# Output turned by VectorE in 32 by 32 blocks instead of by TensorE, with a reordered start and a last sum in halves

## The chip, the cores and the metric

The kernel runs on one core of one Trainium2 chip. The metric is the device time of one execution in microseconds (us), the median of several runs. Three runs of the kernel before took 2236.97, 2237.91 and 2240.64 us; the median is 2237.91 us. In the profiles PE is TensorE's matrix multiply, PEld its weight load, DVE is VectorE, ACT is ScalarE, POOL is GpSimd and SP is SyncE, whose queue here carries most of the transfers.

## The reference, cut to what matters

The input `x` has 32 batches of 512 nodes with 256 features, `adj` has a 512 by 512 mask of zeros and ones for each batch. All is float32.

```
h = relu(layernorm(x))                        # per node, over 256 features
# branch 1: convolution along the nodes
c = relu(bn1(conv1(h)))                       # 1 tap, 256 -> 256
x_conv = relu(bn2(conv2(c)) + h)              # 17 taps, 256 -> 256
# branch 2: messages over a graph
s = h @ w_se.T + b_se                         # 3 numbers per node
A = exp(-|s_n - s_m|^2) * adj
x_nmp = A @ relu(h @ w_msg.T + b_msg)
# gates
x_in = concat(x_conv, x_nmp)                  # 512 features
gi, gh = x_in @ w_ih.T + b_ih,  h @ w_hh.T + b_hh    # three parts each: r, z, n
r = sigmoid(gi_r + gh_r);  z = sigmoid(gi_z + gh_z)
n = tanh(gi_n + r * gh_n)
out = x + (1 - z) * n + z * h
```

## The kernel before, in words

**Layout.** Nearly everything is held turned: features on the 128 partitions (so two halves, d or o = 0 and 1), the 512 nodes along the free axis. The input arrives with nodes on partitions; after the layer norm `norm_t` turns it by TensorE (`turn`, a multiplication with an identity matrix) into `hT`, which is also stored to `HD` in DRAM and fetched again when other stages need it (`hTg` for the graph, `hTb` for the gates, `hT` for a later first convolution).

**Stages per batch.** `norm`: VectorE's statistics, `rsqrt` with a power on GpSimd, `shift` on VectorE, then ScalarE scales the input in place. `norm_t`, then `conv1` into the array `h1`. `convolution`: the 17 taps for a group of 4 batches, as 25 products with transformed weights; the weights are made once, in the first group, from `conv2_w` by `weights_first` on VectorE and ScalarE, and stored to `WD`; later groups fetch them. Operands come from `operand_some` on VectorE. `graph`: `messages`, `kernel_exp`, `masked` (which turns the mask: by TensorE for the first 8 batches; for the others the mask is loaded in 32 by 32 blocks, already moved to their places, and VectorE transposes each block), `gather`. `gates`: four accumulations in PSUM for each half o (`ps_r`, `ps_h`, `ps_z`, `ps_n`), and at the end the mixing of `n`, `z` and `hT` (`mix`, `mix_next`, `mix_last`), which leaves the batch's result, features on partitions, in `o_sb`.

**The output.** `finish` (line 764) takes two of the four blocks of 128 nodes at a time: four `turn`s into one PSUM bank bring nodes back to the partitions, VectorE adds the residual `x` that `load_res` (line 774) has fetched, and SP stores 256 KB in runs of 1 KB. That is 8 turns, 2 additions, 2 stores and 2 residual loads for a batch.

**What sets the order.** The schedule is written out by the program itself. Each stage is a generator in `streams`; a planner keeps a clock `now` of TensorE's planned time and estimates of when VectorE and ScalarE get free (`dve.free`, `act.free`), and always continues the stream that lies furthest back by its own clock. `fill` puts VectorE's background work between (norms, operands, weights, sums), and `LATER` holds small steps with due times. Each engine then runs its instructions in exactly the order in which they were issued, and so does SP's queue with its transfers: an instruction that waits holds up everything behind it on that engine. Before the planner starts, some things are issued outright: the input of batch 0, small vectors, weights, then `bn_affine` twice (scales of the batch norms), then `load(0)`, `load(1)` and so on, which put the norms of the first four batches into `NORMS`, then the convolution weights and the first masks. Weight preparation may begin when the planned clock passes `prepare_at`, 16 there.

Of the kernel before, what the change touches and what calls it, by code (L numbers as in the profile page):

```python
# [8 lines left out]
F32 = mybir.dt.float32  # L9
# [4 lines left out]
P = 128  # L14
# [30 lines left out]
def kernel(  # L45
# [49 lines left out]

    now = 10.0
    LAG = 0.6

    def elements(t):
# [22 lines left out]
    def matmul(ps, lhsT, rhs, **more):  # L124
        nonlocal now
        now += max(0.22, elements(ps) / 600.0)
        nc.tensor.matmul(ps, lhsT, rhs, **more)  # L127

    def turn(ps, a):
        nonlocal now  # L130
        now += 0.11
        nc.tensor.transpose(ps, a, ident)  # L132
# [5 lines left out]
    def bank():  # L138
        return gps.tile([P, N], F32, name="ps_g")
# [4 lines left out]
    def later(t, f):  # L144
        LATER.append((t, f))
        LATER.sort(key=lambda e: e[0])

    def settle():
        while LATER:
            LATER.pop(0)[1]()  # L150


    XS, HT, HB, HR, HG, XN, XR = {}, {}, {}, {}, {}, {}, {}
    NORMS, NORM_AT = {}, {}
    HD = {b: dram.tile([P, ND, N], F32, name=f"hd{b}") for b in range(B)}
    ND_ = {(b, d): dram.tile([P, N], F32, name=f"nd{b}_{d}") for b in range(B) for d in range(ND)}
    begun = 0

    def fetch(b, xs=None):
        XS[b] = front.tile([P, NT, D], F32, name="x_sb", bufs=2) if xs is None else xs  # L160
        nc.sync.dma_start(XS[b], x[b].rearrange("(c p) d -> p c d", p=P))

    def load(b, xs=None):
        if b not in XS:
            fetch(b, xs)
        NORMS[b] = norm(b)
        NORM_AT[b] = now + 7.0 if b >= G else 0.0

    def load_row(b):
        HR[b] = front.tile([P, ND, N], F32, name="hT", bufs=2)  # L170
# [16 lines left out]
            nc.sync.dma_start(XN[b, d], ND_[b, d])  # L187

    fetch(0)
    vec = const.tile([P, _NCOL], F32)  # L190
    nc.sync.dma_start(vec, vecs)
    w1 = const.tile([P, ND, D], F32)
# [7 lines left out]


    wmsg = const.tile([P, ND, D + 3], F32)
    nc.sync.dma_start(wmsg[:, :, :D], w_msg)
    nc.sync.dma_start(wmsg[:, :, D:], w_se)
    bmsg = const.tile([P, D + 3], F32)
    nc.sync.dma_start(bmsg[:, :D], b_msg.to_broadcast([P, D]))
    nc.sync.dma_start(bmsg[:, D:], b_se.rearrange("k o -> o k").to_broadcast([P, 3]))
    ident = const.tile([P, P], F32)
    make_identity(nc, ident)
    mhalf = const.tile([P, 4], F32)  # L210
# [394 lines left out]
                freed = len(X2) // 25  # L605
        return True

    prepare, prepare_at = weights_first(), 16.0

    def prepare_some():  # L610
        nonlocal prepare_at
# [149 lines left out]
        act.activation(sums, ps, AF.Copy)  # L761
        nc.scalar.dma_start(ND_[b, d], sums)

    def finish(b, o_sb, c):
        ps = bank()
        for j in range(2):
            for d in range(ND):
                at = (j * ND + d) * P
                turn(ps[:, at : at + P], o_sb[:, d, (c + j) * P : (c + j + 1) * P])
        y = XR.pop((b, c))  # L770
        dve.tensor_tensor(y, ps.rearrange("p (j d) -> p j d", j=2), y, op=ALU.add)
        nc.sync.dma_start(out[b].rearrange("(c p) d -> p c d", p=P)[:, c : c + 2, :], y)

    def load_res(b):
        for c in range(0, NT if b < B else 0, 2):
            XR[b, c] = late.tile([P, 2, D], F32, name="res", bufs=2)
            nc.sync.dma_start(XR[b, c], x[b].rearrange("(c p) d -> p c d", p=P)[:, c : c + 2, :])

# [54 lines left out]
    def gates(b):  # L835

        load_gates(b)
        load_sums(b, 0)
        load_sums(b, 1)
        hT = HB[b]  # L840
        o_sb = late.tile([P, ND, N], F32, name="o_sb")
        x_in = []

        def cols(o, g):
            return slice(g * D + o * P, g * D + (o + 1) * P)

        def products(ps, o, g, first, last, of, then=None):


            sources = ((whh, 0), (wih, 0), (wih, ND))  # L850
            for k in range(first, last):
                w, at = sources[k]
                for i in range(ND):
                    matmul(
                        ps, w[:, at + i, cols(o, g)], hT[:, i, :] if k == 0 else x_in[2 * k - 2 + i],
                        start=(k == of[0] and i == 0), stop=(k == of[1] and i == ND - 1),
                    )
                if k == last - 1 and then is not None:
                    then()
                yield now  # L860

        def residual():
            xconv = XC.pop(b)[:, :, :N]
            dve.tensor_tensor(xconv, xconv, hT, op=ALU.add)
            yield dve.free + 0.3
            act.activation(xconv, xconv, AF.Relu)
            x_in.extend([xconv[:, i, :] for i in range(ND)] + [XN[b, d] for d in range(ND)])

        def mix_next(r, z, o):
            act.activation(  # L870
                r, r, AF.Tanh,
                bias=vec[:, _COL["b_ih"] + 2 * ND + o : _COL["b_ih"] + 2 * ND + o + 1],
            )
            later(act.free + 0.3, lambda: mix_last(r, z, o))

        def mix_last(r, z, o):
            t = o_sb[:, o, :]
            dve.tensor_tensor(t, hT[:, o, :], r, op=ALU.subtract)
            dve.tensor_tensor(t, z, t, op=ALU.mult)
            dve.tensor_tensor(t, r, t, op=ALU.add)  # L880
            if o == ND - 1:
                unfinished[b] = o_sb

        for o in range(ND):
            r = z = None

            def reset():
                nonlocal r
                settle()
                r = late.tile([P, N], F32, name="r")  # L890
                act.activation(r, ps_r, AF.Sigmoid, bias=brz[:, o : o + 1])

            def reset_hidden():
                dve.scalar_tensor_tensor(
                    r, ps_h, vec[:, _COL["b_hh"] + 2 * ND + o : _COL["b_hh"] + 2 * ND + o + 1], r,
                    op0=ALU.add, op1=ALU.mult,
                )

            def update():
                nonlocal z  # L900
                z = late.tile([P, N], F32, name="z")
                act.activation(z, ps_z, AF.Sigmoid, bias=brz[:, ND + o : ND + o + 1])

            def mix():
                dve.tensor_tensor(r, ps_n, r, op=ALU.add)
                later(dve.free + 0.3, lambda r=r, z=z, o=o: mix_next(r, z, o))
                if o == ND - 1:
                    load_sums(b + 1, 0)
                    load_sums(b + 1, 1)

            ps_r = acc.tile([P, N], F32, name="ps_acc")
            if o == 0:
                yield lambda: b in evacuated
                yield evacuated[b]
                yield from residual()
                yield from products(ps_r, o, 0, 0, 1, (0, 2))
                yield act.free + LAG
            else:
                yield from products(ps_r, o, 0, 0, 1, (0, 2))
            yield from products(ps_r, o, 0, 1, 3, (0, 2), reset)  # L920
            ps_h = acc.tile([P, N], F32, name="ps_acc")
            yield from products(ps_h, o, 2, 0, 1, (0, 0), reset_hidden)
            ps_z = acc.tile([P, N], F32, name="ps_acc")
            yield from products(ps_z, o, 1, 0, 3, (0, 2), update)
            if o == 0:
                load_gates(b + 1)
            ps_n = acc.tile([P, N], F32, name="ps_acc")
            yield from products(ps_n, o, 2, 1, 3, (1, 2), mix)
        gated.add(b)

    unfinished = {}

    def all_finishes():
        for b in range(B):
            yield lambda: b in unfinished
            yield dve.free + LAG
            for c in range(0, NT, 2):
                finish(b, unfinished[b], c)
                yield now
            load_res(b + 1)  # L940


    bn1_sc, bn1_sh = bn_affine("bn1")
    bn2_sc, bn2_sh = bn_affine("bn2")
    brz = const.tile([P, 2 * ND], F32)
    dve.tensor_tensor(
        brz, vec[:, _COL["b_ih"] : _COL["b_ih"] + 2 * ND], vec[:, _COL["b_hh"] : _COL["b_hh"] + 2 * ND],
        op=ALU.add,
    )

    turn_of = 0

# [58 lines left out]

    def all_gates():
        yield lambda: late is not None
        load_res(0)
        for b in range(B):
            yield from gates(b)

# [1 line left out]


    streams = {
        "finish": (all_finishes(), 1e9, -2.0),
        "rows": (all_rows(), 1e9, -2.0),
        "begins": (all_begins(), 4.2, -0.15),
        "graphs": (all_graphs(), 49.0, 0.0),
# [5 lines left out]
    hold = {name: None for name in streams}  # L1031

    load(0)
    load(1)
    spare = front.tile([P, NT, N], F32, name="at", bufs=1).rearrange("p c (k d) -> p (c k) d", d=D)
    for b in (2, 3):
        load(b, spare[:, (b - 2) * NT : (b - 1) * NT, :])
    for k0, k1 in ((0, 9), (9, TAPS)):
        for c in range(ND):
            nc.sync.dma_start(wflat[:, c, k0 + 1 : k1 + 1, :], conv2_w[:, c, k0:k1, :])  # L1040
    gr.ask(3)

# [72 lines left out]
```

## Time and profile before

| what | before |
|---|---|
| median of three runs | 2237.91 us |
| the profiled execution, whole | 2241.54 us |
| its span, first to last instruction | 2239.7 us |
| TensorE busy | 2154.9 us (96%) |
| VectorE busy | 1450.3 us (65%) |
| ScalarE busy | 787.7 us (35%) |
| mean granted TensorE clock | 0.989 |
| DMA: packets, of them under 512 bytes | 328,270, 214,160 |
| first matrix work on TensorE | at 15.1 us |
| first product of the convolution | at 69.2 us |

Busy time is the time in which an engine executes something; where TensorE's work is queued densely, its records overlap. A row of a group gives line, engine, operation, output and inputs, shapes and count, then busy time and mean, then the idle time of that engine just before and who ended it. Since nearly all instructions are issued through helpers, one line (L118) stands for all of VectorE and ScalarE, L127 for all matmuls and L132 for all turns; the names of the tiles tell them apart.

### The profile page before, as it was taken

The numbers are of one execution on the slowest core, as the hardware profiler recorded it, in microseconds if no ns is written. First come the engines' busy times: TensorE is split into PE (matmuls) and PEld (weight loads), VectorE is DVE, ScalarE is ACT, GpSimd is POOL, SyncE is SP. The second block draws the span as 40 slices with busy tenths as digits, with TensorE's granted clock in tenths as the row PEclk, the third lists the DMA queues.
The fourth block names the chain that finished last, engine by engine and source line by source line (L and its number), as shares of the span: only waits on it lengthen the run. The fifth ranks groups of instructions, "written<-read, shape, count | busy, mean of one in ns | idle before, by whom it ended". The sixth has DMA issues, their size and how long they took to land. (4 is left out here: it accounts for less than half of the span.)

```text
span 2239.7 us, 26162 instructions
## 1 busy us (share of the span) xinstructions
PE 2154.9 (96%) x9640; PEld 1346.7 (60%) x9640; DVE 1450.3 (65%) x2700; ACT 787.7 (35%) x1322; POOL 56.7 (3%) x73
## 2 busy tenths in 40 slices
PE   4899899999999999999999999999999999999998
PEld 2777766566655666566665655656666566665443
DVE  4687876666657667568764667747767467676222
ACT  4545532424333342234432343332432324222311
POOL 1000000000000000000000000000000000000000
PEclk9999999999999999999999999999999999999999
DMA  6344645445555455444555445545544544453121
GB/s 237 132 143 178 248 172 190 137 151 157 165 165 160 138 171 178 149 140 151 185 161 182 127 142 161 176 166 174 156 150 151 150 151 145 147 169 85 61 75 37
DMA packets 328270, 342.40 MB, mean 153 GB/s; under 512 B 214160, under 2 KB 263696, under 8 KB 327504
## 3 DMA queue, kind: packets, MB, share of 16 engines
q1 hardware_dynamic: 308720, 287.52, 41.7%
q10 hardware_dynamic: 17424, 46.67, 5.4%
q0 software_dynamic: 2000, 6.56, 0.8%
q8 instruction: 76, 1.25, 0.2%
q14 instruction: 50, 0.41, 0.1%
HBM read 270.68 MB, written 69.99 MB: 152 GB/s over the span
## 5 line engine op out<-in xcount | busy, mean ns | idle before, releaser
L127 PE MATMUL ps_acc<-xconv,wih 128*128 128x512 f32 x768 | 362.4, 594 | 5.2 <-ACT xconv L118 5.2
L127 PE MATMUL ps_acc<-xnb,wih 128*128 128x512 f32 x768 | 363.9, 596 | 0.0
L127 PE MATMUL ps_acc<-hTb,whh 128*128 128x512 f32 x768 | 357.7, 594 | 2.8 <-ACT r L118 2.7
L127 PE MATMUL ps_c<-xd,w 128*128 128x116 f32 x2800 | 342.1, 275 | 0.0
L127 PEld LDWEIGHTS ps_c<-xd,w 128*128 128x128 f32 x2800 | 328.4, 192 | 5.1 <-issue 4.8
L118 DVE TENSOR_TENSOR r<-ps_acc,r 128x512 f32<-128x512 f32 x64 | 44.2, 691 | 392.6 <-PE ps_acc L127 392.6
L127 PEld LDWEIGHTS ps_acc<-xconv,wih 128*128 128x128 f32 x768 | 140.8, 190 | 160.3 <-issue 150.0
L127 PEld LDWEIGHTS ps_acc<-xnb,wih 128*128 128x128 f32 x768 | 140.4, 190 | 156.4 <-issue 155.6
L127 PE MATMUL ps_g<-at,msg 128*128 128x512 f32 x512 | 229.2, 596 | 3.7 <-DVE at L118 3.7
L127 PEld LDWEIGHTS ps_acc<-hTb,whh 128*128 128x128 f32 x768 | 140.3, 190 | 150.2 <-issue 139.0
L127 PEld LDWEIGHTS ps_b<-x,w 128*128 128x128 f32 x1400 | 182.9, 193 | 72.2 <-issue 57.2
L127 PE MATMUL ps_b<-x,w 128*128 128x116 f32 x1400 | 184.9, 275 | 9.4 <-DVE w L118 5.1
L118 ACT ACTIVATE mid<-ps_b 128x232 f32<-128x232 f32 x175 | 63.6, 364 | 318.8 <-PE ps_b L127 301.4
L127 PEld LDWEIGHTS ps_g<-at,msg 128*128 128x128 f32 x512 | 95.7, 191 | 114.7 <-issue 107.4
L118 DVE SCALAR_TENSOR_TENSOR x<-x,x 128x480 f32<-128x480 f32 (+1 forms) x184 | 143.9, 782 | 3.0
L127 PE MATMUL ps_g<-hT,w 128*128 128x512 f32 x256 | 122.5, 622 | 22.1 <-ACT hT L118 11.4
L127 PE MATMUL ps_g<-wmsg,hTg 128*128 128x259 f32 x512 | 131.8, 389 | 4.8 <-ACT h L118 4.5
L118 DVE TENSOR_TENSOR x<-x 128x240 f32<-128x240 f32 (+1 forms) x320 | 134.3, 461 | 0.4
L118 DVE SCALAR_TENSOR_TENSOR r<-ps_acc,vec,r 128x512 f32<-128x512 f32 x64 | 48.0, 750 | 123.3 <-PE ps_acc L127 108.2
L127 PEld LDWEIGHTS ps_g<-wmsg,hTg 128*128 128x128 f32 x512 | 96.5, 194 | 47.2 <-issue 29.7
L118 ACT ACTIVATE h<-ps_g,bn_shift,bn_scale 128x252 f32<-128x252 f32 (+1 forms) x192 | 81.0, 495 | 119.2 <-PE ps_g L127 118.0
L118 DVE TENSOR_TENSOR msg<-ps_g,bmsg 128x256 f32<-128x256 f32 x128 | 53.5, 419 | 103.6 <-PE ps_g L127 103.2
(101 smaller groups left out, 2437.3 us busy)
## 6 DMA issues: line engine op xcount, KB each, us to landing
w<-wd SPq DMA_DIRECT2D x150, 768.0 KB, 5.2
m_sb<-in_adj_dram SPq DMA_DIRECT2D x384, 64.0 KB, 2.5
hd<-hT ACTq DMA_DIRECT2D x32, 512.0 KB, 4.9
hTg<-hd SPq DMA_DIRECT2D x32, 512.0 KB, 4.5
res<-in_x_dram SPq DMA_DIRECT2D x64, 256.0 KB, 3.2
hTb<-hd SPq DMA_DIRECT2D x32, 512.0 KB, 5.9
xnb<-nd SPq DMA_DIRECT2D x64, 256.0 KB, 2.8
out_dram<-res SPq DMA_DIRECT2D x64, 256.0 KB, 2.3
```

Source lines behind the costliest of these rows:

```text
L118: getattr(self.engine, name)(*tiles, **more)
L127: nc.tensor.matmul(ps, lhsT, rhs, **more)
```

## The change

The output is no longer turned by TensorE. `leave` replaces `finish`: for each half o, VectorE transposes the 128 by 512 result within blocks of 32 by 32, adds the residual, and four transfers store it, each moving 32 partitions with runs of 128 bytes (32 features of one node). The residual is loaded in the same arrangement, four transfers for each half, into a ring of three buffers. The blocks' order along the rows is set by the DRAM side of these transfers. `r` has two buffers now, `o_sb` holds one half instead of two.

At the start, the input of batch 1 is asked for right behind that of batch 0; the whole norm of batch 0 is issued before the `bn_affine` scales; message weights are asked for after the inputs of the first four batches; the two parts of the convolution weights come in another order; the planner's clock begins at 5 and weight preparation may begin at 26 instead of 16.

At the end, the last accumulation of the last batch (`ps_n`, o = 1) is done in two halves of 256 columns, and mixing, transposing and storing are done for each half.

```diff
-    now = 10.0
+    now = 5.0
...
+    ARRIVES = (0.0, 7.0, 11.0, 13.0)
...
-        NORM_AT[b] = now + 7.0 if b >= G else 0.0
+        NORM_AT[b] = now + 7.0 if b >= G else ARRIVES[b]
...
     fetch(0)
+    fetch(1)
...
-    prepare, prepare_at = weights_first(), 16.0
+    prepare, prepare_at = weights_first(), 26.0
...
-    def finish(b, o_sb, c):
-        ps = bank()
-        for j in range(2):
-            for d in range(ND):
-                at = (j * ND + d) * P
-                turn(ps[:, at : at + P], o_sb[:, d, (c + j) * P : (c + j + 1) * P])
-        y = XR.pop((b, c))
-        dve.tensor_tensor(y, ps.rearrange("p (j d) -> p j d", j=2), y, op=ALU.add)
-        nc.sync.dma_start(out[b].rearrange("(c p) d -> p c d", p=P)[:, c : c + 2, :], y)
...
+    XB = x.rearrange("b (k i) d -> b i k d", i=32)
+    OB = out.rearrange("b (k i) d -> b i k d", i=32)
+
+    def blocks(t, dram_b, o, store):
+        for g in range(P // 32):
+            at = o * P + 32 * g
+            a = t[32 * g : 32 * g + 32, :].rearrange("i (k j) -> i k j", j=32)
+            d = dram_b[:, :, at : at + 32]
+            nc.sync.dma_start(*((d, a) if store else (a, d)))
+
+    def load_res(b, o):
+        if b < B and (b, o) not in XR:
+            XR[b, o] = late.tile([P, N], F32, name="res", bufs=3)
+            blocks(XR[b, o], XB[b], o, False)
...
+        def mix_last(r, z, o, s):
+            if s.start == 0:
+                parts.append(late.tile([P, N], F32, name="o_sb"))
+            t = parts[-1]
+            dve.tensor_tensor(t[:, s], hT[:, o, s], r[:, s], op=ALU.subtract)
+            dve.tensor_tensor(t[:, s], z[:, s], t[:, s], op=ALU.mult)
+            dve.tensor_tensor(r[:, s], r[:, s], t[:, s], op=ALU.add)
+            later(dve.free, lambda: leave(r, t, o, s))
+
+        def leave(r, t, o, s):
+            dve.transpose(t[:, s], r[:, s])
+            y = XR[b, o]
+            dve.tensor_tensor(y[:, s], t[:, s], y[:, s], op=ALU.add)
+            for g in range(P // 32):
+                at = slice(32 * g, 32 * g + 32)
+                nc.sync.dma_start(
+                    OB[b][:, s.start // 32 : s.stop // 32, o * P + 32 * g : o * P + 32 * g + 32],
+                    y[at, s].rearrange("i (k j) -> i k j", j=32),
+                )
+            if s.stop == N:
+                del XR[b, o]
+                load_res(b + 1, o)
...
-                r = late.tile([P, N], F32, name="r")
+                r = late.tile([P, N], F32, name="r", bufs=2)
...
-            yield from products(ps_n, o, 2, 1, 3, (1, 2), mix)
+            if b < B - 1 or o < ND - 1:
+                yield from products(ps_n, o, 2, 1, 3, (1, 2), mix)
+                continue
+
+            for h in range(2):
+                s = slice(h * N // 2, (h + 1) * N // 2)
+                for j in range(2 * ND):
+                    matmul(
+                        ps_n[:, s], wih[:, j, cols(o, 2)], x_in[j][:, s],
+                        start=(j == 0), stop=(j == 2 * ND - 1),
+                    )
+                mix(s)
+                yield now
+            settle()
...
     load(0)
+    while 0 in NORMS:
+        NORM_AT[0] = next(NORMS[0], -1.0)
+        if NORM_AT[0] < 0.0:
+            del NORMS[0]
+    bn1_sc, bn1_sh = bn_affine("bn1")
+    bn2_sc, bn2_sh = bn_affine("bn2")
...
+    NORM_AT[0] = act.free + LAG
     load(1)
...
+    nc.sync.dma_start(wmsg[:, :, :D], w_msg)
...
-    for k0, k1 in ((0, 9), (9, TAPS)):
-        for c in range(ND):
+    for c in range(ND):
+        for k0, k1 in ((0, 9), (9, TAPS)):
             nc.sync.dma_start(wflat[:, c, k0 + 1 : k1 + 1, :], conv2_w[:, c, k0:k1, :])
```

More of the change, by code (lines that the diff above doesn't have):

```diff
@@ L202 @@
     wmsg = const.tile([P, ND, D + 3], F32)
-    nc.sync.dma_start(wmsg[:, :, :D], w_msg)
-    nc.sync.dma_start(wmsg[:, :, D:], w_se)
     bmsg = const.tile([P, D + 3], F32)
-    nc.sync.dma_start(bmsg[:, :D], b_msg.to_broadcast([P, D]))
-    nc.sync.dma_start(bmsg[:, D:], b_se.rearrange("k o -> o k").to_broadcast([P, 3]))
     ident = const.tile([P, P], F32)
@@ L762, in gather @@
         nc.scalar.dma_start(ND_[b, d], sums)
-    def finish(b, o_sb, c):
-        ps = bank()
-        for j in range(2):
-            for d in range(ND):
-                at = (j * ND + d) * P
-                turn(ps[:, at : at + P], o_sb[:, d, (c + j) * P : (c + j + 1) * P])
-        y = XR.pop((b, c))
-        dve.tensor_tensor(y, ps.rearrange("p (j d) -> p j d", j=2), y, op=ALU.add)
[L772 to L777, printed above, removed]
+    XB = x.rearrange("b (k i) d -> b i k d", i=32)
[10 more added lines that the diff above has]
+            blocks(XR[b, o], XB[b], o, False)
     def begin(b):
@@ L840, in gates @@
         hT = HB[b]
-        o_sb = late.tile([P, ND, N], F32, name="o_sb")
+        parts = []
         x_in = []
@@ L867, in residual, with mix_next @@
             x_in.extend([xconv[:, i, :] for i in range(ND)] + [XN[b, d] for d in range(ND)])
-        def mix_next(r, z, o):
+        def mix_next(r, z, o, s):
             act.activation(
-                r, r, AF.Tanh,
+                r[:, s], r[:, s], AF.Tanh,
                 bias=vec[:, _COL["b_ih"] + 2 * ND + o : _COL["b_ih"] + 2 * ND + o + 1],
             )
[L874 to L882, printed above, removed]
+            later(act.free + 0.3, lambda: mix_last(r, z, o, s))
+        def mix_last(r, z, o, s):
[19 more added lines that the diff above has]
+                load_res(b + 1, o)
         for o in range(ND):
@@ L902, in update, with mix @@
                 act.activation(z, ps_z, AF.Sigmoid, bias=brz[:, ND + o : ND + o + 1])
-            def mix():
-                dve.tensor_tensor(r, ps_n, r, op=ALU.add)
-                later(dve.free + 0.3, lambda r=r, z=z, o=o: mix_next(r, z, o))
+            def mix(s=slice(0, N)):
+                dve.tensor_tensor(r[:, s], ps_n[:, s], r[:, s], op=ALU.add)
+                later(dve.free + 0.3, lambda r=r, z=z, o=o: mix_next(r, z, o, s))
                 if o == ND - 1:
@@ L927, in gates @@
             ps_n = acc.tile([P, N], F32, name="ps_acc")
-            yield from products(ps_n, o, 2, 1, 3, (1, 2), mix)
-        gated.add(b)
[L931 to L949, printed above, removed]
+            if b < B - 1 or o < ND - 1:
[11 more added lines that the diff above has]
+            settle()
+        gated.add(b)
     turn_of = 0
@@ L1013, in all_gates @@
         yield lambda: late is not None
-        load_res(0)
+        for o in range(ND):
+            load_res(0, o)
         for b in range(B):
@@ L1021 @@
     streams = {
-        "finish": (all_finishes(), 1e9, -2.0),
         "rows": (all_rows(), 1e9, -2.0),
@@ L1033 @@
     load(0)
+    while 0 in NORMS:
[4 more added lines that the diff above has]
+    bn2_sc, bn2_sh = bn_affine("bn2")
+    brz = const.tile([P, 2 * ND], F32)
+    dve.tensor_tensor(
+        brz, vec[:, _COL["b_ih"] : _COL["b_ih"] + 2 * ND], vec[:, _COL["b_hh"] : _COL["b_hh"] + 2 * ND],
+        op=ALU.add,
+    )
+    NORM_AT[0] = act.free + LAG
     load(1)
@@ L1037 @@
         load(b, spare[:, (b - 2) * NT : (b - 1) * NT, :])
-    for k0, k1 in ((0, 9), (9, TAPS)):
-        for c in range(ND):
+    nc.sync.dma_start(wmsg[:, :, :D], w_msg)
+    nc.sync.dma_start(wmsg[:, :, D:], w_se)
+    nc.sync.dma_start(bmsg[:, :D], b_msg.to_broadcast([P, D]))
+    nc.sync.dma_start(bmsg[:, D:], b_se.rearrange("k o -> o k").to_broadcast([P, 3]))
+    for c in range(ND):
+        for k0, k1 in ((0, 9), (9, TAPS)):
             nc.sync.dma_start(wflat[:, c, k0 + 1 : k1 + 1, :], conv2_w[:, c, k0:k1, :])
```

## The prediction

> **What bounds the kernel now.** First the page: span and busy shares; then the table of stages, the groups with shapes kept apart, the chain that ended last, and the timeline of the start.
>
> ```profile
> span 2239.7 us, 26162 instructions
> PE 2154.9 (96%) x9640; PEld 1346.7 (60%) x9640; DVE 1450.3 (65%) x2700; ACT 787.7 (35%) x1322; POOL 56.7 (3%) x73
> 0.00:69.20 69.20, 34.74 (x109) 19.41 (x110) 31.86 (x100) 36.22 (x74) 10.27 (x22) 0.92 0.57 215
> 69.20:130.00 60.80, 55.26 (x402) 49.60 (x401) 46.67 (x99) 25.26 (x43) 2.31 (x2) 0.95 0.35 126
> 130.00:280.00 150.00, 138.87 (x891) 111.61 (x891) 125.33 (x228) 75.03 (x139) 7.36 (x10) 0.97 0.56 200
> 700.00:2097.00 1397.00, 1379.22 (x6066) 849.28 (x6065) 930.48 (x1697) 483.54 (x790) 17.30 (x14) 1.00 0.50 153
> ```
>
> The stage rows give the stretch, its length, then busy PE, weight load, VectorE, ScalarE, GpSimd, clock, DMA share, GB/s. From 700 to 2097 us TensorE lacks 18 of 1397 us: work taken off TensorE there is time saved. In the first 69.2 us it lacks 34.5, and no other engine is full: that stage is waits.
>
> Groups by shape (busy, mean ns | idle before), then two pieces of the chain:
>
> ```profile
> L132 PE MATMUL ps_g<-ident,o_sb 128*128 128x128 f32 x256 | 33.3, 272 | 3.6 <-DVE o_sb L118 3.6
> L118 DVE STREAM_TRANSPOSE right<-m_sb 128x512 f32<-128x512 f32 x96 | 67.6, 704 | 27.8 <-PE ps_g L734 22.3 <-DMA hTb<-hd 3.5 <-issue 1.8
> 2169.14 0.87 PE ps_g L132 x8
> 2202.47 0.87 PE ps_g L132 x8
> ```
>
> The timeline of the start (start, length, [idle before]), then a row of the DMA issues (KB each, us to land) and one of SP's waits:
>
> ```profile
> 14.44 2.07 ACT L118 ACTIVATE x_sb<-x_sb,shift,rstd 128x256 f32<-128x256 f32 x4 [8.60 <-DVE shift L118]
> 23.02 1.76 DVE L118 SCALAR_TENSOR_TENSOR g<-wraw 128x1536 f32<-128x1536 f32 x1 [8.61 <-DMA wraw<-in_conv_w_dram]
> 26.49 0.15 DVE L118 SCALAR_TENSOR_TENSOR shift<-mv,rstd 128x4 f32<-128x4 f32 x1
> 28.30 5.08 PE L127 MATMUL ps_g<-hT,w 128*128 128x512 f32 x8 [10.40 <-ACT hT L118]
> 69.23 12.24 PE L127 MATMUL ps_c<-x,w 128*128 128x116 f32 x96
> m_sb<-in_adj_dram SPq DMA_DIRECT2D x384, 64.0 KB, 2.5
> SPq L772 <- DVE res L118: 263.6, 39, 28.8
> ```
>
> To see: the 256 output turns; eight of them take 0.87 us of the chain; the same 32-block transpose already runs on VectorE for masks (704 ns); VectorE's queue stood behind a convolution weight not yet landed (23.02) while batch 1's `shift` waited behind it until 26.49, and with it TensorE until 28.30; the convolution begins at 69.23.
>
> **What the skill says.** "Perfetto Trace Analysis", Identifying the Most-Contended Engine: matmul busy time overstates, as matmuls overlap. The trace agrees: each turn is recorded at 272 ns, but eight pass in 0.87 us, 109 ns each. I use the pace. "VectorE: DVE Perf Modes", The three transpose paths: VectorE transposes only within 32x32 blocks. So the blocks' places must be set by the DMA, which is why the runs shrink to 128 bytes. "DMA: Bandwidth & Descriptors", Specifications: under 512 B a transfer is below line rate, through read-modify-write. For loads the trace shows it mildly: in its packet records a 128-byte mask packet takes 13 ns and a 1 KB packet 52, half the rate per byte. No run here shows 128-byte stores. "Trainium Kernel Development and Optimization", Key Constraints: the SP, ACT and POOL queues share 16 DMA engines; the page's queues add to 48% of them.
>
> **The change part by part.**
>
> *Turns removed.* 32 batches x 8 turns at 0.87 us per eight: -27.8 us, all within stages where TensorE has no gaps. With them go the PSUM banks of `finish` and TensorE's waits for them (1.1 us); left out.
>
> *VectorE adds.* 64 transposes x 704 ns = 45 us; the residual add stays (682 ns from PSUM before; 691 ns is what 128x512 adds from SBUF take). VectorE goes from 1450 to 1495 of some 2200 us, 68%. I cost it at nothing: VectorE's idle third covers it. Without cover it costs at most the 45 us; queued behind these 1.4 us are operands, weight sums and evacuations, made at least a product ahead. TensorE's waits on VectorE sum to some 14 us; I allow +1 us for more.
>
> *Loads and stores.* 64 residual loads and 64 stores become 256 each of 64 KB (the last store is 8 of 32 KB): 384 more on SP's queue, net of four. A mask load of this shape takes 486 ns to issue, so +187 us of SP, which idles most of the time. Now, per batch, SP issues two stores (0.99), waits for landing (1.2) and issues two loads (1.1): 3.3 us. After, twice a batch, 8 issues: 3.9 us. The third `res` buffer takes the landing wait away. Behind them stand the loads of `w`, masks, `hT`, `xnb`; `w` is fetched two products ahead (some 20 us), which covers 4. Packets: 131,072 loads x 13 ns replace 16,384 x 52, +0.85 ms of engine time; stores at an unknown x. From below, x is the load's 13 ns; from above a 1 KB packet's 52, since a partial write may cost a full one; I take 40. Then stores add 131,072 x 40 ns less 0.85 = 4.4 ms. The sum of 5.2 ms over 16 engines is 330 us each: 48% busy becomes some 63%. Cost: round trips like `hT` stored and fetched lengthen. TensorE waited 8.8 us there in two places; I allow +2 us.
>
> *Start.* Batch 0's input is there at 4.56 in both. Before, 3.1 us of batch-norm scales and then batch 1's statistics (landed only at 11.9) stood ahead of batch 0's `shift`. Now: statistics 2.25 us, epsilon 0.17, GpSimd 1.0, `shift` at 8.3, ScalarE 8.45, first turn 9.1 instead of 15.1: 6 us. Batch 1's input is asked for second, its `shift` follows the scales (3.1) and statistics of batches 1 and 2 (4.5) at 16.2 instead of 26.5; no weight preparation stands ahead, that now comes after batch 4's statistics. A new wait: TensorE's order puts messages of batch 0 (12 records) ahead of convolution 1 of batch 1, and these need `hTg`. hT is stored at 12.4, +4.9 to land, fetched at 17.5 and landed +4.5 at the least, later since SP's queue holds 4.4 MB of `wraw` and 0.8 MB of masks ahead; at the 407 GB/s of 10 to 20 us everything asked before it (near 8 MB) is in by 24. So messages 24.5 to 28, convolution 1 of batch 1 until 32. From there ScalarE is the bound: three pairs of evacuations (2.6 each) 7.8, messages 1.3, normalising 4.2, `hT` copies 2.8, small ones 0.8 = 17, +2 for issues and gaps: h of batch 3 at 49 to 50, VectorE's first operands 2.5 later, convolution at 53 instead of 69.2. I carry 15 of these 16 us, since weights then come from VectorE, 77 to 84% busy up to 280. Bounds: +3 (messages later, nothing carried) to -21.
>
> *Last sum in halves.* TensorE's time is equal. After its end (T = 2230.82) the kernel now takes 8.8 us. New: half add 0.44 (a 128x256 add from PSUM is 419 ns), six half operations of 0.45, transpose and add 0.85 for the first half: T+4.0, second T+4.9. SP's eight issues from T+4.0 at 0.31 to 0.49 put the last at T+6.2 to 7.4; the last store now takes 3.3 from issue to end: T+9.5 to 10.7. So the halves win about what eight small issues lose: +1.2, between -0.5 and +2.
>
> Sum: -27.8 - 15 + 1 + 2 + 1.2 = -38.6. The profiled execution took 2241.5 (span 2239.7); 2241.5 - 38.6 = 2202.9. The median of the runs is 3.6 lower: **2199 us**, 1.7% faster.
>
> **Rivals.**
>
> *Only the turns count (chance 0.15).* The start moves, but preparing weights on VectorE sets the pace up to 280 us. For: VectorE is 84% busy from 130 to 280. Against: its 32 us of work before 69 are also moved forward. 2237.9 - 27.8 + 4.2 = 2214.
>
> *Late loads (0.14).* SP stands before a store whose VectorE add is not done, as it did for 263.6 us, and loads behind slip, on busier DMA engines. One such slip cost 4.4 us (8.8 in two places); in six of the 28 `hT` loads it costs 26: 2225. Against: stores and loads per batch took SP 3.3 us in one place before too.
>
> *Slow stores (0.05), ends slower.* Read-modify-write makes 128-byte stores so dear that DMA bounds. The engines have 35.8 ms in all and use 17.2; stores cross the rest at 18.6 ms / 131,072 = 142 ns. At 200 ns the load is 17.2 + 26.2 = 43.4 ms, 2711 us. Against: three times my upper price. For: no store of that size was seen.
>
> *The change does not act (0.02).* The engines' orders show the turns gone, so only with the gain lost elsewhere: 2238.
>
> **How the numbers follow.** My case has 0.64, with its own range 2181 to 2214 (start -21 to -3, VectorE and loads 0 to +8, tail -0.5 to +2). With the first two rivals the range is 2181 to 2226. Faster: 0.64 + 0.15 + 0.14 = 0.93; same 0.02; slower 0.05. A change of 0.2% (4.5 us) is about what a measurement of this kernel can tell from none.
>
> **What would show it.** Right: no `o_sb` turns on TensorE, its busy time 28 to 33 us less; 160 transposes of 704 ns on VectorE; first turn near 9 us, first `ps_c` near 53; SP's wait for stores gone from the `res` loads; DMA share near 0.6; end 9 to 11 us after the last matmul. Wrong: a first `ps_c` after 62, a stage from 700 to 2100 with more than 35 us of idle TensorE, or `out_dram` landing far over 2.5 us.

## The result: slower, not faster

The changed kernel takes 2250.86 us (median, 2247.76 to 2254.52), the kernel before 2237.64 us (median of four runs): a ratio of 1.0057, 95% interval 1.0039 to 1.0075. Forecast were 2199 us, with a range from 2181 to 2226. The profiled execution of the changed kernel took 2247.76 us, 6.2 us more than that of before (2241.54).

The page of the changed kernel, its heads and SP's queue (q1):

```profile
span 2246.0 us, 26120 instructions
...
PE 2128.4 (95%) x9392; PEld 1320.0 (59%) x9392; DVE 1494.8 (67%) x2770; ACT 787.1 (35%) x1323; POOL 56.0 (2%) x73
...
DMA packets 563856, 342.42 MB, mean 152 GB/s; under 512 B 482512, under 2 KB 499280, under 8 KB 563088
...
q1 hardware_dynamic: 544304, 287.54, 47.0%
```

The table of stages of the changed kernel (stretch, length, then busy PE, weight load, VectorE, ScalarE, GpSimd, clock, DMA share, GB/s):

```profile
0.00:69.20 69.20, 38.38 (x124) 22.13 (x125) 38.29 (x113) 35.77 (x73) 9.99 (x22) 0.83 0.57 215
69.20:130.00 60.80, 54.82 (x398) 48.01 (x398) 39.96 (x84) 27.95 (x48) 2.62 (x2) 0.95 0.39 139
130.00:280.00 150.00, 137.78 (x883) 109.92 (x883) 126.66 (x230) 72.91 (x134) 7.90 (x11) 0.98 0.58 199
280.00:700.00 420.00, 403.95 (x1781) 249.48 (x1780) 278.19 (x528) 141.60 (x244) 18.42 (x24) 0.98 0.55 158
700.00:2097.00 1397.00, 1360.17 (x5898) 831.29 (x5897) 963.42 (x1744) 482.66 (x791) 17.04 (x14) 0.99 0.56 153
```

TensorE's busy time fell by 26.5 us without the turns, a little less than the 28 to 33 forecast; its mean granted clock was 0.983 against 0.989. Its idle time rose from 84.8 (2239.7 - 2154.9) to 117.6 us. In the stage from 700 to 2097 us, where it had lacked 17.8 us, it now lacks 36.8; from 280 to 700 us it lacks 16.0, before 2.9 (417.12 us busy). The turns are gone, and waits have come in their place. TensorE's own waits in the changed kernel (total us, times, longest) name them:

```profile
PE ps_g L127 <- DMA hT<-hd: 31.1, 5, 9.9
PE ps_b L127 <- DMA w<-wd: 13.2, 9, 3.4
...
PE ps_g L127 <- issue: 10.9, 1, 10.9
...
PE ps_acc L127 <- DMA xnb<-nd: 2.3, 3, 1.4
```

Before, `w` and `xnb` were not in the list, and `hT` cost less:

```profile
PE ps_g L127 <- DMA hT<-hd: 8.8, 2, 4.6
```

So +22.3, +13.2 and +2.3: 37.8 us of waiting for loads. The row that ends in "issue" (a wait for which the profile names no cause) is in the start: the messages, which came too early.

What the turns became, in the groups with shapes kept apart, and the same end of the chain that showed 0.87 us for each eight turns before:

```profile
L118 DVE STREAM_TRANSPOSE o_sb<-r 128x512 f32<-128x512 f32 x63 | 44.4, 705 | 0.6
```

```profile
2140.85 29.47 PE ps_acc L127 x68
2173.30 29.47 PE ps_acc L127 x68
2205.76 27.76 PE ps_acc L127 x68
```

A transpose takes 705 ns, and no turn stands in the chain between its accumulations. The new transfers themselves land quickly; their rows of the DMA issues (KB each, us to land):

```profile
res<-in_x_dram SPq DMA_DIRECT2D x256, 64.0 KB, 2.4
...
out_dram<-res SPq DMA_DIRECT2D x252, 64.0 KB, 2.0
```

Before, with 256 KB each, they took 3.2 and 2.3 us. Of the loads that TensorE now waits for, `hT` lands no later (4.8 us, before 5.1), `w` and `xnb` a little later (5.5 against 5.2, 3.4 against 2.8). A wait for `w` takes 1.5 us on average, for `hT` 6.2. By these medians `hT` and mostly `w` come late because they are issued late; for `xnb`, 2.3 us in all, the longer landing can be the cause.

### One stall, followed back

SP's queue in the changed kernel ahead of the stall from 934 to 942 us (start, us for the group, line, transfer, count):

```profile
914.62 2.04 SPq L892 DMA_DIRECT2D out_dram<-res  x4
916.71 2.91 SPq L772 DMA_DIRECT2D res<-in_x_dram  x4
919.72 16.17 SPq L264 DMA_DIRECT2D m_sb<-in_adj_dram  x8
935.99 0.43 SPq L469 DMA_DIRECT2D w<-wd  x1
936.52 0.38 SPq L172 DMA_DIRECT2D hT<-hd  x1
```

The eight mask loads just before, at 907.98, took 5.36 us; these take 16.17. SP's waits between 905 and 970 us say why, and TensorE's timeline what it cost:

```profile
SPq L264 <- DMA nd<-right: 9.9, 1, 9.9
```

```profile
941.96 5.88 PE L127 MATMUL ps_g<-hT,w 128*128 128x512 f32 x8 [7.48 <-DMA hT<-hd]
```

A mask load reads an input and writes a buffer that no `nd` touches, yet it waits 9.9 us for ScalarE's store of `nd`. The order of the changed kernel's instructions with the waits that each carries shows how (SP's queue, 149 to 158; then one of ScalarE's):

```
149 L892 DMACopy out_dram<-res 32x16x32 [waits DMAHW2_49,DVE_49]
150 L892 DMACopy out_dram<-res 32x16x32 [waits DMAHW3_49]
151 L892 DMACopy out_dram<-res 32x16x32 [waits DMAHW4_49]
152 L892 DMACopy out_dram<-res 32x16x32 [waits DMAHW5_49]
153 L772 DMACopy res<-in_x_dram 32x16x32 [waits DMAHW7_49]
154 L772 DMACopy res<-in_x_dram 32x16x32 [waits DMAHW0_49]
155 L772 DMACopy res<-in_x_dram 32x16x32 [waits DMAHW1_49]
156 L772 DMACopy res<-in_x_dram 32x16x32 [waits DMAHW2_49]
157 L469 DMACopy w<-wd_210 128x1536 [waits DMAHW3_49,DMASW6_49,PE_49]
158 L469 DMACopy w<-wd_211 128x1536 [waits DMAHW4_49,DMASW7_49,PE_49]

175 L760 DMACopy nd_0_116<-right 128x512 [waits DMAHW1_49,Activation_49]
```

Completion is counted on eight counters, DMAHW0 to 7, dealt out in turn to SP's and ScalarE's transfers together, and each transfer waits until the one eight before it has landed: 157 waits for 150. Between 152 and 153 number 6 is missing; it went to a transfer of ScalarE. In the stall above it is the same: of the eight mask loads the second waits for number 7, dealt to a store of `nd`, the fourth for number 1, dealt to a store of `hd`, and the seventh for number 4, dealt to the other store of `nd`. SP's waits from 905 to 970 us have all three, 9.9, 1.1 and 1.0 us. GpSimd's transfers count on others (DMASW). So a store of ScalarE that is dealt its counter but still waits for TensorE's gather stops SP at the eighth transfer after it. The Trainium skill, "DMA: Bandwidth & Descriptors", Anatomy of one DMA, states in its account of GpSimd's path that DMA engines do not wait on semaphores and that the wait happens on the issuing sequencer; the trace agrees for SP, which stands still for 9.9 us, with all that is queued behind it.

SP's waits in the whole of the changed kernel (total us, times, longest):

```profile
SPq L892 <- DVE res L118: 263.7, 42, 15.3
...
SPq L264 <- DMA nd<-right: 80.6, 9, 10.5
SPq L892 <- DMA nd<-right: 72.8, 10, 9.6
```

All of SP's waits that stores of `nd` or `hd` ended add to 312 us, against 187 before. The wait for VectorE's sum is what it was, 263.7 against 263.6. Of the five stalls on `hT` (named here by their ends), three (at 665, 942 and 1216 us, 25.2 us in all) have such a wait of 9.5 to 9.9 us for `nd` in front; two (424 and 967 us, 5.9 us in all) have a store that waited for VectorE and then its eight transfers.

### The profile page after: what moved, and what is told of

It reads as the page before. It is cut to its first block, busy times and chain, and to the rows that moved or that the text cites. A ratio compares the mean times of both kernels' runs of the same rounds, so it can differ in the third digit from the quotient of the medians.

```text
span 2246.0 us, 26120 instructions
## 1 busy us (share of the span) xinstructions
PE 2128.4 (95%) x9392; PEld 1320.0 (59%) x9392; DVE 1494.8 (67%) x2770; ACT 787.1 (35%) x1323; POOL 56.0 (2%) x73
## 4 chain that ended last, share of the span: by engine, by line
PE 85%; DMA 6%; DVE 4%; ACT 2%; issue 1%; SPq 1%; ACTq 0%; POOL 0%; DVEq 0%; POOLq 0%
PE ps_acc L127 41%; PE ps_g L127 19%; PE ps_c L127 15%; PE ps_b L127 6%; DMA w<-wd 2%; PE ps_g L132 2%; PE ps_b L732 1%; DMA hT<-hd 1%; DMA nd<-at 1%; DMA xnb<-nd 1%; DMA hd<-hT 1%; ACT at L118 1%; DVE gg L118 1%; DVE x L118 0%; DVE xconv L118 0%
## 5 line engine op out<-in xcount | busy, mean ns | idle before, releaser
L127 PE MATMUL ps_acc<-xconv,wih 128*128 128x512 f32 (+1 forms) x772 | 362.8, 592 | 5.7 <-ACT xconv L118 5.2
L127 PE MATMUL ps_acc<-xnb,wih 128*128 128x512 f32 (+1 forms) x772 | 362.9, 592 | 2.3 <-DMA xnb<-nd 2.3
L118 DVE TENSOR_TENSOR r<-ps_acc,r 128x512 f32<-128x512 f32 (+1 forms) x65 | 44.4, 683 | 385.6 <-PE ps_acc L127 385.6
L127 PE MATMUL ps_b<-x,w 128*128 128x116 f32 x1400 | 184.9, 275 | 23.4 <-DMA w<-wd 13.2
L127 PE MATMUL ps_g<-hT,w 128*128 128x512 f32 x256 | 126.7, 641 | 32.8 <-DMA hT<-hd 31.1
L127 PE MATMUL ps_g<-wmsg,hTg 128*128 128x259 f32 x512 | 130.4, 388 | 11.4 <-issue 10.9
L127 PEld LDWEIGHTS ps_g<-wmsg,hTg 128*128 128x128 f32 x512 | 96.7, 194 | 54.3 <-issue 41.7
```

Of the source, the lines that this page charges most:

```text
L118: getattr(self.engine, name)(*tiles, **more)
```

## Experiments

Two theories at first. **Shared counters:** loads are late because SP waits for ScalarE's unfinished stores, the more often the more transfers it gives out. **SP's own time:** loads are late because more transfers stand in front of them. Against both, slow 128-byte stores: these were already out, since a packet of 128 bytes takes 13 ns in the records (median), and as much in the last 12 us, where all packets of this size are stores.

### The parts alone

The first kernel has the change of the output alone, with the start of before and the last sum whole (it leaves out the mixing and the storing of the last half of the last batch); the second has the start alone. The first lines by which the old start is put back:

```diff
-    fetch(1)
...
-    prepare, prepare_at = weights_first(), 26.0
+    prepare, prepare_at = weights_first(), 16.0
```

> The changed output (VectorE transposes, 128-byte runs) alone: start as before, last sum whole. Theory L (late loads through shared completion counters: SP's and ScalarE's transfers take eight counters in turn, and each transfer waits for the one eight before it) and its rivals P (128-byte packets slow the DMA engines) and S (SP's own time for 384 more issues) all place the loss in the output: about 2250 us, since the changed start gave about 5 us. Theory Q (the changed start and the plan that follows from it cause the late loads): about 2212 us, the turns' 27.8 us less than before.

> The changed start alone: output turned by TensorE and stored in 1 KB runs as before. L, P and S: the first product of the convolution about 5 us earlier and nothing lost later, about 2233 us. Q: stalls on hT and w as in the changed kernel, 2255 us or more.

Measured: output alone 2248.67 us, ratio 1.0039 (1.0027 to 1.0051); start alone 2237.78, ratio 1.0000 (0.9992 to 1.0009). The output carries the loss (what this kernel leaves out would only add to its time), and the start brings nothing by itself. The complete changed kernel with the old start is below.

TensorE's waits with the start alone:

```profile
PE ps_g L127 <- issue: 11.8, 1, 11.8
```

### ScalarE's stores moved to GpSimd's queue

The 96 stores of `hd` and `nd`, in the changed kernel and in the kernel before:

```diff
-            nc.scalar.dma_start(HD[b], HT[b])
+            nc.gpsimd.dma_start(HD[b], HT[b])
...
-        nc.scalar.dma_start(ND_[b, d], sums)
+        nc.gpsimd.dma_start(ND_[b, d], sums)
```

> The changed kernel with ScalarE's 96 stores of hT and of the message sums issued from GpSimd's queue, which has its own completion counters; SP's issues, their number and all packets stay. L: SP no longer waits for stores that ScalarE has yet to issue; the stalls of TensorE on hT, w and xnb (46.6 us) fall below 12, about 2215 us. P: nothing changes, 2251. S: nothing changes, 2251.

> The kernel before with the same 96 stores moved to GpSimd's queue. L: the kernel before lost some time to the same wait (8.8 us on hT): about 2228 us. P and S: the same as before, 2238. If GpSimd's queue delays the norms behind a waiting store, slower than before; then the run of the changed kernel with it is read against this one.

Measured: changed 2202.71 us, ratio to the kernel before 0.9845 (0.9831 to 0.9858); before 2224.36, ratio 0.9948 (0.9935 to 0.9961). The same edit is worth 48.2 us in the changed kernel and 13.6 in the one before. Stages and TensorE's waits of the changed kernel with moved stores:

```profile
280.00:700.00 420.00, 414.79 (x1834) 256.46 (x1833) 286.72 (x542) 145.81 (x254) 29.15 (x44) 0.99 0.56 163
700.00:2097.00 1397.00, 1382.52 (x5942) 840.17 (x5941) 968.76 (x1750) 488.27 (x794) 49.64 (x72) 1.00 0.57 154
```

```profile
PE ps_g L127 <- DMA hT<-hd: 11.1, 5, 4.0
PE ps_g L127 <- issue: 9.2, 1, 9.2
```

SP's waits for stores of `nd` and `hd` fall from 312 to 25.7 us; `w` is out of the list. TensorE's waits for loads fall from 46.6 to 11.1 us, and its busy time by another 8.2 (2128.4 to 2120.2) for the same work. That ScalarE has 96 transfers less to issue is not what helps: TensorE's waits for ScalarE add to 38.8 us without the move and 39.1 with it. The edit changes the issuing engine together with the counters; that it works through the counters is read from SP's waits and from the order of instructions, and the two were not tried apart. With the stores moved in both kernels, the change as a whole is worth -21.7 us.

### Extra small loads on SP

If only the number of transfers matters, the kernel before can be made slow by 384 loads of 4 KB that nobody needs, six behind each store of the output:

```diff
+    def pad(c):
+        for k in range(6):
...
+            nc.sync.dma_start(PAD[c, k][:32, :], x[0, :32, :32])
```

> The kernel before, output by TensorE in 1 KB runs, with six loads of 4 KB into unused tiles behind each of the 64 stores: 384 more transfers on SP's queue, as many as the change adds, but 12,288 small packets instead of 262,144 and no work moved on any engine. L (shared completion counters used up sooner): SP's waits that end with a store of ScalarE (nd and hd) rise from 187 us to 300 or so, TensorE stalls on hT, and the time is 2250 us or more. P (128-byte packets): 2238. That the plan without turns leaves loads less lead (Q'): 2238.

> The kernel before with 384 extra 4 KB loads on SP's queue, and its hd and nd stores given out by GpSimd instead of ScalarE. If the extra loads cost 34 us only because they use up completion counters that SP shares with ScalarE's late stores, they cost next to nothing here: 2224 to 2230 us, with the idle time of TensorE in front of ps_g that hT ended near the 2.4 us of the kernel before with moved stores. If it is SP's own issue time (384 more instructions on that queue, or its own ring of counters), the 34 us stay: about 2258 us, and that idle time stays near 30 us.

Measured: 2273.55 us, ratio 1.0145 (1.0131 to 1.016); with `hd` and `nd` stored from GpSimd 2263.11, ratio 1.0105 (1.009 to 1.012). So the loads cost 34.2 us with shared counters (2239.31 in that comparison) and 38.8 without. The theory that extra transfers cost only by way of ScalarE's stores has fallen, and SP's waits for those stores had hardly risen in the first of the two (187 to 192 us). What costs is seen in SP's queue of the second, ahead of a stall of 8.45 us at 1211.58:

```profile
1196.69 0.39 SPq L772 DMA_DIRECT2D out_dram<-res  x1
1197.13 3.84 SPq L780 DMA_DIRECT2D pad<-in_x_dram  x6
1201.07 0.41 SPq L772 DMA_DIRECT2D out_dram<-res  x1
1201.52 2.79 SPq L780 DMA_DIRECT2D pad<-in_x_dram  x6
1204.35 0.94 SPq L785 DMA_DIRECT2D res<-in_x_dram  x2
1205.45 0.35 SPq L171 DMA_DIRECT2D hT<-hd  x1
```

```profile
PE ps_g L127 <- DMA hT<-hd: 24.4, 6, 8.4
```

Twelve transfers of 4 KB hold SP for 6.6 us between a store that had waited for VectorE and the load of `hT`; that load has no such slack (the time between its usual landing and its first use). The wait for `hT` goes from 2.4 us (stores moved, no extra loads) to 24.4. It is the place that counts more than the number: the changed kernel with moved stores has as many transfers added, eight at a time, and waits 11.1 us for `hT`.

### Residual loads off SP

So the transfers of the change itself were taken out of SP's line, with ScalarE's stores left where they are, and in the best kernel so far (below):

```diff
-            nc.sync.dma_start(*((d, a) if store else (a, d)))
+            nc.gpsimd.dma_start(*((d, a) if store else (a, d)))
```

> The changed kernel (2250.9 us) with nothing but its 256 residual loads given to GpSimd's queue; hd and nd stores stay on ScalarE's queue and share the counters with SP. With the stores moved and the first messages late, taking the residual loads off SP was worth 10 us. If all that they cost is their own issue time in front of the hT loads, 2241 us. If they cost as much again by bringing SP sooner to the transfer that waits for a late store of ScalarE, 2225 to 2235 us, and SP's waits ended by stores of nd or hd fall well under the 312 us of the changed kernel. If the waits for ScalarE's stores only move on to the next transfer on SP, 2248 to 2252 us with those waits still about 312 us.

> The changed kernel with hd and nd stores on GpSimd's queue and the first messages planned later (2192.2 us), and the residual loads given to GpSimd's queue too, which takes 256 transfers and their waits for VectorE's buffers off SP's queue. If what is left of TensorE's idle time in front of ps_g (about 12 us in all) comes from SP standing before a residual load, it goes: 2182 to 2189 us. If it comes from elsewhere, 2191 to 2193 us. If GpSimd's queue now holds a store of hd or nd behind a residual load that waits for its buffer, loads of hT are late again: 2200 us or more.

Measured: 2218.27 us, ratio 0.9905 (0.9889 to 0.9922), 32.6 us less than the changed kernel; and 2182.22, ratio 0.9743 (0.9729 to 0.9756), 10.0 less than without the edit, as expected if SP stood before these loads. TensorE's waits of the first, and SP's:

```profile
PE ps_g L127 <- DMA hT<-hd: 21.8, 5, 10.1
...
PE ps_g L127 <- issue: 10.3, 1, 10.3
```

```profile
SPq L264 <- DMA nd<-right: 80.5, 11, 9.0
SPq L892 <- DMA nd<-right: 79.0, 11, 9.6
```

None of the three expectations for the first came out. It gained more than SP's own time alone should give, while SP's waits for ScalarE's stores stayed at 299 us in all, against 312. Yet far less of them reaches TensorE: `w` is down from 13.2 to 1.0 us, `hT` from 31.1 to 21.8. The two causes are not additive. Our reading is that waits for ScalarE and transfers in front add up to one lateness of SP's line, and that TensorE pays what exceeds the slack of each load; the slack of each load was not measured. The edit also takes these 256 transfers out of the shared counters, which was not tried apart.

### The start and the tail

The start of before in the changed kernel, complete this time, and the same with ScalarE's stores moved:

> The changed kernel with the start of before; the output and the halved last sum stay, and everything is computed. The run with the output alone left out the mixing and the store of the last half of the last batch, so its 2248.7 us is some 8 us short. If the start is worth nothing (as 2237.8 against 2237.9 says), 2251 to 2257; if the start cost time within the changed kernel, below 2248.

> The changed kernel with ScalarE's stores on GpSimd's queue and the start of before. Against the kernel before with those stores moved (2224.4 us) it holds the output and the halves alone: by the turns' 27.8 us, and 1 to 4 given back on loads and at the end, 2198 to 2201. If the start is worth its 3 to 5 us of earlier convolution even here, it would be that much slower than 2202.7 us.

Measured: 2257.17 us, ratio 1.0072 (1.0059 to 1.0085), and 2200.66, ratio 0.9825 (0.9811 to 0.9838). The new start saves 6.3 us in the changed kernel and costs 2.1 once the stores are moved. The kernel before itself differed by up to 1.7 us between the comparisons (2237.64 to 2239.31), so the 2.1 are hardly more than nothing. Why so little, the timeline of the changed kernel's start shows:

```profile
9.24 2.80 PE L132 MATMUL ps_g<-ident,x_sb 128*128 128x128 f32 x8 [9.24 <-ACT x_sb L118]
...
12.70 0.34 ACTq L318 DMA_DIRECT2D hd<-hT  x1
...
21.22 0.33 SPq L177 DMA_DIRECT2D hTg<-hd  x1
...
31.88 1.63 PE L127 MATMUL ps_g<-wmsg,hTg 128*128 128x259 f32 x3 [10.90 <-issue]
```

The first turn comes at 9.24 us, 5.9 earlier. But `hT`, stored at 12.70, takes 8.5 us to land and can be fetched only at 21.22, and the fetch that serves the messages takes another 10.6 us (3.3 in the kernel before), while the DMA engines move 397 to 409 GB/s. TensorE stands 10.9 us and ScalarE behind it; the first convolution product comes at 64.28. So the messages were planned later:

```diff
-            yield now + 9.0
+            yield now + (22.0 if b < 1 else 9.0)
```

> The changed kernel with ScalarE's stores on GpSimd's queue and the plan's delay for the first batch's messages 22 instead of 9, so that TensorE does the first convolutions of batches 1 to 3 before it needs hTg, which in the changed kernel landed 10.6 us after its issue, behind the weights. If that wait (9.2 us) held up the start: first product of the convolution near 57 instead of 65.8 us and 2195 us. If the start is set by something else by then: 2203.

> The changed kernel with hd and nd stores on GpSimd's queue and the first messages planned later (2192.2 us), and the last sum of the last batch whole again. The prediction put the halves at +1.2 us of tail: if that is right, about 2191 us, with some 8.8 us from the last matmul to the end instead of about 10. If halves overlap the last store with the last sum, it is slower by about 1 us.

Measured, both with ScalarE's stores moved: 2192.22 us, ratio 0.979 (0.9777 to 0.9804), 10.5 less than without; and with the last sum whole 2191.21, ratio 0.9782 (0.9769 to 0.9796). TensorE's timeline of the former:

```profile
55.41 5.23 PE L127 MATMUL ps_c<-x,w 128*128 128x116 f32 x32
```

The convolution starts 10.4 us earlier than with the messages early in otherwise the same kernel (65.82), and the whole is 10.5 us shorter. The halves differ by 1.0 us from the whole sum, within what these runs can tell; in one profile each, the time from the last matmul to the end is 10.2 us with halves and 9.8 with the whole sum.

The medians of output, start and queues side by side, in us:

| kernel | `hd`, `nd` stored from ScalarE | from GpSimd |
|---|---|---|
| before | 2237.64 | 2224.36 |
| before, 384 extra loads | 2273.55 | 2263.11 |
| changed, old start | 2257.17 | 2200.66 |
| changed | 2250.86 | 2202.71 |
| changed, residual loads on GpSimd | 2218.27 | not tried |
| changed, messages late | not tried | 2192.22 |
| changed, both of these | not tried | 2182.22 |

The best of all, with stores and residual loads on GpSimd's queue and the messages late, is the 2182.22 us above: 2.6% under the kernel before. TensorE's wait for `hT` there:

```profile
PE ps_g L127 <- DMA hT<-hd: 4.9, 4, 2.0
```

## Why the prediction was wrong

*Turns removed, -27.8:* right in kind and roughly in size. With the old start and the stores moved, the changed output and tail take 2200.66 us against 2224.36 for the kernel before with moved stores: -23.7. The steps for turns, VectorE, loads and tail add to -27.8 + 1 + 2 + 1.2 = -23.6. That the two meet is in part luck: between these kernels TensorE's busy time fell by 30.4 us (2145.2 to 2114.8), and its waits for `hT` rose by 9.2 (11.6 against 2.4), where the step for loads had 2.

*VectorE adds, +1:* right. TensorE's waits on VectorE add to 11.2 us, 15.1 before.

*Loads and stores, +2:* **this is the step that failed.** It weighed the new transfers against the lead of `w`, some 20 us, which did not hold (nine waits for `w`, 13.2 us), and allowed 2 us for the others. It priced SP's 3.9 us twice a batch about rightly (1.97 and 2.12 us for four stores and four loads at 959 us) but took SP to be idle most of the time, where what counts is SP's lateness at the one load of `hT` in a batch, which had little slack before (8.8 us of waits). And it missed that SP's transfers share their counters with ScalarE's. In the changed kernel the loads cost 37.8 us of waiting where 2 were allowed. Its price for a stored packet, 40 ns of a bracket from 13 to 52, was wrong as well and harmless: 13 ns, at the lower end; q1's share went from 41.7 to 47.0%, not to some 57.

*Start, -15:* wrong by itself, too. First turn at 9.1 forecast, 9.24 measured; messages at 24.5 forecast, 31.88 measured. It was the round trip of `hT` that was sized too small: 8.5 us to store and 10.6 to fetch, where 4.9 and at least 4.5 were put, while the DMA engines were fully busy (share 1.01 to 1.05 from 15 to 30 us). The wait behind it shifted everything on ScalarE. The convolution came at 64.28, not 53; with that wait taken away by a later plan, at 55.41.

*Last halves, +1.2:* from the end of the last accumulation to the end of the span it takes 10.0 us, 8.8 before. The medians (+1.0) do not contradict it, but the whole sum with the new output takes 9.8 too, so little of the difference belongs to the halves; the sign is not settled.

Does the sum close? Forecast -38.6, measured +13.2, so 51.8 us are to be found. Having these stores on ScalarE's queue cost the changed kernel 48.2 us and the one before 13.6: 34.6 new. The start with stores moved is +2.1 where -15 was booked: 17.1. Together 51.7. That it closes so exactly is luck, given what the medians of different comparisons can tell (1.7 us) and the offsetting terms above. The division depends on the order in which parts are undone: the residual loads taken off SP recover 32.6 of the same microseconds.

*Rivals.* Only the turns count (0.15, 2214 us) was right that the start brings nothing by itself, but not for its reason: with the same preparation of weights, planning the messages later gained 10.5 us. That the change does not act (0.02) is out: the turns are gone. Late loads (0.14, 2225 us) had the right kind of event. Its place was only part of it: stores that waited for VectorE stood before two of the five stalls on `hT`, 5.9 of 31.1 us. Its size, 26 us, was near the rise on `hT` (22.3) but left out `w`, and the start was taken as won. Slow stores did not happen. The range ended at 2226 because no case let two steps fail together, and slower was tied to slow stores alone. Of the signs named for a wrong forecast two came: first `ps_c` after 62, and more than 35 us of idle TensorE from 700 to 2097 (36.8).

## What to carry to other kernels

Price an added transfer by where it stands in its queue: list what is behind it, and how long before its use each load there is issued; the mean idle time of the queue says little. Look in the instruction order for transfers that wait for a completion counter held by another engine's queue, since then a store that is merely early in program order stops loads that have nothing to do with it. Where a change looks good on the compute engines and a load is the only thing late, try giving its neighbours to another queue before dropping the change.

## What the runs showed that was not expected

- Which queue gives out a transfer mattered by up to 48 us in 2251, at the same traffic. The Trainium skill, "DMA: Bandwidth & Descriptors", Issuing engines are not separate DMA queues, says that several issuing engines save only the sequencer's time, usually small. Here the choice was worth more, since what went was mostly SP's waiting: 96 stores moved gave 48.2 and 13.6 us, 256 loads moved 32.6 and 10.0.
- A stall costs more than its length. After the 7.48 us at 934, eight matmuls took 5.88 us, where 3.6 is usual, at half the clock. The stages around it in the changed kernel (the last three figures are the granted clock, DMA share and GB/s):

```profile
931.00:934.00 3.00, 3.00 (x24) 2.54 (x23) 0.00 (x0) 0.96 (x2) 0.00 (x0) 1.00 0.72 179
934.00:942.00 8.00, 0.52 (x6) 0.36 (x4) 0.00 (x0) 0.00 (x0) 0.00 (x0) 0.85 0.89 269
943.00:945.00 2.00, 2.00 (x4) 0.96 (x3) 0.00 (x0) 0.00 (x0) 0.00 (x0) 0.50 0.99 407
```

  "TensorE: Matmul & The Clock Gate", Part 1, has an idle window of some 3.4 us halve the clock; the trace agrees, with 0.50 after 7.5 us, and after the 2.18 us stall at 967 eight matmuls took the usual 3.67.
- Stores in runs of 128 bytes cost no more than loads of that size, 13 ns a packet; no read-modify-write shows in their time.
